# Summing the softmax denominators of the last attention unit: GpSimd adds replaced by accumulating DMAs

## The chip, the cores and the metric

The kernel is one program on one NeuronCore of a Trainium2 chip. Its time is the device time of one execution in microseconds (us). The kernel before takes 1054.57 us, the median of 3 runs (1052.63 to 1055.07). The engines are TensorE (PE in the profile, its weight loads PEld), VectorE (DVE), ScalarE (ACT), GpSimd (POOL) and SyncE (SP, which only issues DMAs here).

## The reference: what is computed

One transformer block in float32 on x of shape (2, 1024, 512): attention with 16 heads of 32 and low-rank additions to its four weight matrices, residual, layer norm, then a mixture-of-experts feed-forward layer (8 experts of 704 hidden units, 256 slots each, and a shared one), residual, layer norm. What matters here is the attention's core:

```
scores = jnp.einsum('bhqd,bhkd->bhqk', q, k) * SCALE
attn = jax.nn.softmax(scores, axis=-1)
out = jnp.einsum('bhqk,bhkd->bhqd', attn, v)
```

The softmax divides by the sum of the exponentials over all 1024 keys. The kernel applies this division after the product with v: it sums the exponentials beside it and scales the product.

## The kernel before

**Units and steps.** Attention's second pass is cut into 16 units (NU): a unit is 4 heads and 512 queries. A unit has 8 steps of 128 keys, so there are 128 steps; step t belongs to unit t // 8. In step t, st_step (L611) does for each of the 4 heads one matmul of scores (L620, 128 keys x 512 queries) and on ScalarE its exponential (L629). The exponentials of two heads, a pair, share one tile of 128 x 1024, pts[t, pair]. In the same step, av_step(t - 1) (L633) multiplies the exponentials of the step before with v (L639), adding up in one PSUM bank over the unit's eight steps. The tiles pts come from a pool of 14 buffers (PTB). The first pass (L189, L197), which finds row maxima, runs 12 steps ahead of the second and so is over by step 116.

**The denominators.** They need the sum of pts over the 8 steps and over the 128 partitions. Matmuls with a matrix of ones do the sum over partitions (finish, L666, matmuls at L672), and what of the eight tiles has been added together before saves such matmuls. The adds are spread by a table, ADDS (L62), by unit and step within the unit; adds(t) (L648) is called in step t + 1, right after av_step(t). A word of the table has two letters, for pair 0 and pair 1, and the number of a tile: b makes this tile the accumulator, v adds it to the accumulator on VectorE, p does that on GpSimd, and d starts a DMA that adds the tile into the next one:

```
accs[u, pr] = pts[i, pr]                                                    # b
pool.dma_start(out=pts[i + 1, pr], in_=pts[i, pr], accum_op=ALU.add)        # d, L656
eng.tensor_tensor(accs[u, pr], accs[u, pr], pts[i, pr], ALU.add)            # v, p: L659
```

Such an accumulating DMA is issued by GpSimd and moves 512 KB between tiles in SBUF. It may start when the value matmuls have read the tile that it adds into. Tile 7 of a unit is not added: finish sums it directly (DIRECT), in all units but unit 14 (NO_DIR).

In unit 15, the last, table row NU - 1 makes tile 0 the accumulator (step 121); pair 0 of tiles 1 to 5 is added by VectorE and pair 1 by GpSimd (steps 122 to 126); VectorE adds both pairs of tile 6 (step 127). In unit 14 tile 1 is the accumulator, tiles 0, 2 and 4 go into their neighbours by DMA, and VectorE adds tiles 3, 6, 7 and 5, the last three in step 120.

**What follows a sum.** For units 13 to 15 (RDIR) finish takes VectorE's reciprocal of the sums (L682, 128 x 512). normalize (L706) then has three parts: VectorE scales the product (L711), a copy is rounded for the projection (L714 on VectorE for units 13 and 14, L716 on ScalarE for unit 15), VectorE takes the rest (L718). FINE and NRME (L78) set the step within unit 15 at which unit 14's finish and normalize are queued: steps 123 and 125. In finish's step the sum comes on TensorE after av_step, and its reciprocal on VectorE after adds. In normalize's step the first part stands ahead of that step's adds and the other two behind them.

**The end of attention.** After step 127 come av_step(127), adds(127), finish(15), the first part of normalize(15), and then the output projection of rows 0 to 127 of the second batch element (op10, L744), which needs unit 14 but not unit 15. The list TAIL (L83) sets the order behind it: rows 128 to 511 (o1 to o3) also need only unit 14, rows 512 to 1023 (o4 to o7) unit 15 too. In between, ScalarE rounds and GpSimd splits the shared expert's weights (s0 to s5, L562 and L568), whose tiles two buffers feed (loads by SyncE, L554: a load waits for the split two before it), and GpSimd sets up the router (w0, L470). Behind that the feed-forward layer runs to the end.

**Order.** All engines' instructions stay in the order in which the program writes them (manual_schedule with MAN2), each engine with a queue of its own. An instruction that waits holds up all behind it on its engine.

Of the kernel before, what the change touches and what calls it, by code (L numbers as in the profile page):

```python
# [20 lines left out]
NU = 16  # L21
# [41 lines left out]
    None: {0: "bb0", 2: "dd1", 3: "pp3", 4: "pp4", 5: "pp2", 6: "pp5", 7: "pp6"},  # L63
    NU - 3: {0: "bb0", 2: "dd1", 3: "pp3", 4: "pp4", 5: "pp2", 7: "dd6 pp5"},
    NU - 2: {1: "bb1 dd0", 3: "dd2", 5: "dd4", 6: "vv3", 7: "vv6 vv7 vv5"},
    NU - 1: {0: "bb0", 1: "vp1", 2: "vp2", 3: "vp3", 4: "vp4", 5: "vp5", 6: "vv6"},
}
OPROJ_AT = (65, 67, 69, 71, 73, 75, 77, 79)
RES_AT = tuple(8 * i + (2 if i % 2 else 6) for i in range(8)) + (70, 74, 86, 90, 100, 102, 106, 110)
# [5 lines left out]
W2_AT = {2: (0, 1), 3: (2, 3), 4: (4,), 5: (5,)}  # L75
MPJ, MPP = 0, 2
RDIR = NU - 3
FINE, NRME = 3, {NU - 2: 6, NU - 1: 5}  # L78
OPROJ1 = 0
NRM_DVE = (NU - 3, NU - 2)  # L80
ROOT_LAG, NORM_LAG = 1, 4
# [1194 lines left out]
```

## Time and profile before

| what | value |
|---|---|
| median of 3 runs | 1054.57 us |
| the profiled execution | 1057.79 us |
| its span, first to last instruction | 1056.1 us |
| its granted TensorE clock, mean | 0.992 |
| PE, DVE, ACT, POOL busy | 1030.1, 696.0, 527.1, 585.9 us |
| second pass of attention, first to last score matmul | 155.6 to 601.5 us |
| VectorE adds L659 from unit 14's first (575.6) on | 15 |
| GpSimd adds L659 in unit 15, first start and last end | 585.14 and 600.8 us |
| accumulating DMAs L656 in the whole kernel | 36 (median 6.4 us from issue to landing) |

Lines of a timeline are start, duration, engine, line of the code, operation, output<-input, shapes and the number of instructions merged into the row; in brackets stands how long the engine had been idle and who ended that. Tiles are named without numbers: pt is any pts, sm a sum, av a product with v, rc a reciprocal, op a projection. A score or value matmul of float32 shows as one or two passes (x). In the table of stretches each engine has its busy time with the number of instructions, and PEclk is the granted share of TensorE's full clock.

### The profile page before, as it was taken

What the parts mean: (1) busy time and instruction counts of PE and PEld (TensorE: products, weight loads), DVE (VectorE), ACT (ScalarE), POOL (GpSimd) and SP (SyncE); (2) the same over time, 40 slices, a digit from 0 to 9 for tenths busy, and PEclk for the clock granted to TensorE, in tenths of its full rate; (3) what the DMA queues carried; (4) which work ended last, traced back from release to release, by engine and by line L of the source; (5) the groups of instructions that cost most, each with busy time, mean ns of one, the idle gap of its engine ahead of it and who ended that gap; (6) DMA issues with size and microseconds to landing.
All of it is one profiled execution on the core that took longest, in us unless ns stands there. A gap on an engine that the chain in (4) does not pass through costs nothing. (4 is left out here: it accounts for less than half of the span.)

```text
span 1056.1 us, 16556 instructions
## 1 busy us (share of the span) xinstructions
PE 1030.1 (98%) x5994; PEld 742.5 (70%) x5994; DVE 696.0 (66%) x1191; ACT 527.1 (50%) x1023; POOL 585.9 (55%) x407
## 2 busy tenths in 40 slices
PE   8999999999999999999999889999999999999995
PEld 6888774444444456544444359899999999999994
DVE  7732788778888877778887974233522557777752
ACT  5422216666666655566666716222222447555552
POOL 4000006999999986979995655000050046766674
PEclk9999999999999999999999989999999999999998
DMA  9866863454646553535648123000073456777721
GB/s 294 278 225 212 253 194 91 91 135 104 137 93 148 119 127 81 126 85 123 146 115 184 21 60 111 21 21 20 21 244 107 130 175 232 254 249 245 259 84 60
DMA packets 85449, 149.83 MB, mean 142 GB/s; under 512 B 15428, under 2 KB 24132, under 8 KB 85368
## 3 DMA queue, kind: packets, MB, share of 16 engines
q1 hardware_dynamic: 76344, 117.31, 37.5%
q0 software_dynamic: 9024, 31.48, 12.4%
q8 instruction: 47, 0.77, 0.3%
q14 instruction: 34, 0.28, 0.1%
HBM read 95.83 MB, written 33.78 MB: 123 GB/s over the span
## 5 line engine op out<-in xcount | busy, mean ns | idle before, releaser
L197 DVE TENSOR_REDUCE mt<-s 128x1 f32<-128x512 f32 x512 | 323.9, 681 | 79.7 <-PE s L189 79.3
L659 POOL TENSOR_TENSOR pt<-pt,pt 128x1024 f32<-128x1024 f32 x143 | 350.7, 2918 | 6.7 <-ACT pt L629 6.4
L629 ACT ACTIVATE pt<-st 128x512 f32<-128x512 f32 x512 | 269.1, 602 | 130.4 <-PE st L620 117.0
L620 PE MATMUL st<-qs,ks 98*128 98x512 f32 x512 | 213.2, 427 | 1.7 <-ACT pt L629 1.0
L189 PE MATMUL s<-ks,qs 96*128 96x512 f32 x512 | 200.3, 398 | 1.0 <-DVE mt L197 1.0
L620 PEld LDWEIGHTS st<-qs,ks 98*128 98x128 f32 x512 | 95.6, 189 | 133.5 <-issue 93.1
L656 POOL DMA_DIRECT2D pt<-pt x36 | 33.3, 1113 | 174.4 <-PE st L620 165.0
L890 PE MATMUL h<-xthe,w13s 128*128 128x256 f32 x704 | 130.0, 284 | 0.0
L878 POOL TENSOR_TENSOR w2s<-w2r,w2s 128x512 fp32r<-128x512 f32 x42 | 65.9, 1590 | 93.9 <-ACT w2s L877 93.6
L189 PEld LDWEIGHTS s<-ks,qs 96*128 96x128 f32 x512 | 97.1, 190 | 20.3 <-DVE mt L197 5.6
L890 PEld LDWEIGHTS h<-xthe,w13s 128*128 128x128 f32 x704 | 110.7, 191 | 0.3
L890 PE MATMUL h<-xtle,w13s 128*128 128x256 f32 x352 | 100.3, 285 | 0.0
L639 PE MATMUL av<-pt,vt 128*32 128x512 f32 x512 | 75.3, 605 | 0.0
L1038 POOL DMA_INDIRECT xd_d<-x1a,slot_i x8 | 7.9, 984 | 110.4 <-DVE slot_i L1035 108.3
L639 PE MATMUL av<-pt,x1b 128*32 128x512 f32 x512 | 68.2, 605 | 0.0
L890 PEld LDWEIGHTS h<-xtle,w13s 128*128 128x128 f32 x352 | 67.4, 191 | 0.7
L934 PE MATMUL y<-w2s,hs 128*128 128x512 f32 x260 | 60.9, 390 | 0.1
L934 PEld LDWEIGHTS y<-w2s,hs 128*128 128x128 f32 x260 | 48.2, 188 | 10.2 <-DVE hs L916 0.5
L331 ACT ACTIVATE oh<-o,bqk_sb 128x512 fp32r<-128x512 f32 x32 | 22.0, 690 | 57.8 <-PE o L316 53.0
L316 PE MATMUL o<-xh,wh 128*128 128x512 f32 x116 | 45.5, 392 | 0.3 <-DVE ol L332 0.3
L901 ACT ACTIVATE sl<-h 128x256 f32<-128x256 f32 x40 | 15.4, 385 | 60.5 <-PE h L890 59.2
L316 PE MATMUL o<-xh,wl 128*128 128x512 f32 x116 | 45.4, 391 | 0.0
(830 smaller groups left out, 1846.8 us busy)
## 6 DMA issues: line engine op xcount, KB each, us to landing
pt<-pt POOLq DMA_DIRECT2D x36, 512.0 KB, 6.4
x1a<-in_w_dram SPq DMA_DIRECT2D x24, 512.0 KB, 5.1
w2r<-in_w_dram SPq DMA_DIRECT2D x42, 256.0 KB, 3.4
qkd<-oh SPq DMA_DIRECT2D x32, 256.0 KB, 2.4
qkd<-ol SPq DMA_DIRECT2D x32, 256.0 KB, 2.4
x1b<-in_w_dram SPq DMA_DIRECT2D x16, 512.0 KB, 5.6
qs<-qkd SPq DMA_DIRECT2D x30, 256.0 KB, 4.5
ks<-qkd SPq DMA_DIRECT2D x18, 256.0 KB, 4.5
```

Of the source, the lines that this page charges most:

```text
L189: pe.matmul(s1, Qs[u % 3][0:96, h, qt * P : qt * P + P], Ks[g % 2][0:96, h, kh * 512 : kh * 512 + 512], start=True, stop=True,)
L197: dve.tensor_reduce(mts[u][:, c, kh : kh + 1], s1, AX.X, ALU.max)
L316: pe.matmul(o, lhs, rhs, start=k + i == 0, stop=k + i == KC + 1)
L331: act.activation(oh, o, AF.Identity, bias=bias)
L620: pe.matmul(sb, Ks[g % 2][:, h, kc * P : kc * P + P], Qs[u % 3][:, h, :], start=True, stop=True,)
L629: act.activation(pts[t, h // 2][:, h % 2, :], sb, AF.Exp, scale=SCALE)
L639: pe.matmul(avs[u][32 * h : 32 * h + 32, :], vts[g][:, kc, 32 * h : 32 * h + 32], pts[t, h // 2][:, h % 2, :], start=kc == 0, stop=kc == 7 ...
L656: pool.dma_start(out=pts[i + 1, pr], in_=pts[i, pr], accum_op=ALU.add)
L659: eng.tensor_tensor(accs[u, pr], accs[u, pr], pts[i, pr], ALU.add)
L878: pool.tensor_tensor(hl[:, 1, :], raw, f(hl[:, 0, :]), ALU.subtract)
L890: pe.matmul(hp[:, j * 256 : j * 256 + 256], lhs, rhs[:, k, :], start=n == 0, stop=n == 11,)
L934: pe.matmul(o, lhs, rhs, start=n == 0, stop=n == 16)
```

## The change

Row NU - 1 of the table of adds is written anew, and two constants become one step smaller.

```
-    NU - 1: {0: "bb0", 1: "vp1", 2: "vp2", 3: "vp3", 4: "vp4", 5: "vp5", 6: "vv6"},
+    NU - 1: {1: "bb1 dd0", 3: "dd2", 4: "vv4", 5: "vv5", 6: "vv3 vv6"},
...
-FINE, NRME = 3, {NU - 2: 6, NU - 1: 5}
+FINE, NRME = 2, {NU - 2: 6, NU - 1: 4}
```

In unit 15 tile 1 is now the accumulator. In step 122 GpSimd issues two DMAs that add tile 0 into tile 1 (one per pair), in step 124 two that add tile 2 into tile 3. VectorE adds both pairs of tile 4 (step 125), of tile 5 (step 126), and of tiles 3 and 6 (step 127). GpSimd adds nothing in this unit. Unit 14's finish is queued in step 122, its normalize in step 124. Everything else stays.

## The prediction

> **What bounds the kernel now.** I read the page first (TensorE busy 98% of the span), then the stretches around the end of attention:
>
> ```profile
> core 0: us, PE busy (x) PEld busy (x) DVE busy (x) ACT busy (x) POOL busy (x), PEclk, DMA share, GB/s
> 588.00:605.00 17.00, 16.35 (x79) 5.37 (x72) 16.86 (x10) 12.29 (x23) 11.99 (x5) 1.00 0.00 1
> 605.00:618.00 13.00, 6.72 (x19) 3.12 (x20) 10.87 (x5) 1.17 (x2) 9.24 (x28) 0.74 0.28 82
> 618.00:640.00 22.00, 22.00 (x108) 17.98 (x107) 15.71 (x37) 8.31 (x14) 10.21 (x11) 1.00 0.27 84
> ```
>
> Before and after the middle stretch TensorE is full at clock 1.00; in it TensorE works 6.72 of 13 us at clock 0.74, and VectorE is the busy engine. TensorE's waits from 575 to 640 name one cause:
>
> ```profile
> PE sm L672 <- DVE pt L659: 6.9, 3, 4.7
> ```
>
> Those are the denominators' sums (L672) waiting for the adds (L659). TensorE's timeline shows where, and what the idling does to the matmuls behind it:
>
> ```profile
> 589.51 1.05 PE L672 MATMUL sm<-pt,ones 128*32 128x512 f32 x4 [0.38 <-DVE pt L659]
> 590.50 0.73 PE L620 MATMUL st<-qs,ks 98*128 98x512 f32 x2
> ...
> 603.29 1.44 PE L672 MATMUL sm<-pt,ones 128*32 128x512 f32 x5
> 609.40 1.40 PE L672 MATMUL sm<-pt,ones 128*32 128x512 f32 x4 [4.67 <-DVE pt L659]
> 612.68 1.92 PE L672 MATMUL sm<-pt,ones 128*32 128x512 f32 x4 [1.88 <-DVE pt L659]
> 614.54 0.80 PE L744 MATMUL op<-wo_h,at_h 128*128 128x512 f32 x1
> ```
>
> TensorE is through with scores, values and the direct part of unit 15's sum at 604.73 (603.29 + 1.44); then it stands for the accumulator's two halves. The output projection (L744) starts at 614.54. From there to the end TensorE waits 0.3 us in all, so what this place loses or gains goes to the end. VectorE in the same time, then GpSimd:
>
> ```profile
> 575.64 1.22 DVE L659 TENSOR_TENSOR pt<-pt,pt 128x1024 f32<-128x1024 f32 x1
> 579.23 16.86 DVE L659 TENSOR_TENSOR pt<-pt,pt 128x1024 f32<-128x1024 f32 x9 [2.37 <-DMA pt<-pt]
> 596.02 3.34 DVE L682 RECIPROCAL rc<-sm 128x512 f32<-128x512 f32 x1
> 599.29 2.58 DVE L659 TENSOR_TENSOR pt<-pt,pt 128x1024 f32<-128x1024 f32 x1
> ...
> 604.85 7.78 DVE L659 TENSOR_TENSOR pt<-pt,pt 128x1024 f32<-128x1024 f32 x3
> ```
> ```profile
> 575.20 1.75 POOL L656 DMA_DIRECT2D pt<-pt  x2 [4.57 <-PE av L639]
> ...
> 585.14 6.55 POOL L659 TENSOR_TENSOR pt<-pt,pt 128x1024 f32<-128x1024 f32 x2 [5.84 <-ACT pt L629]
> 592.26 8.53 POOL L659 TENSOR_TENSOR pt<-pt,pt 128x1024 f32<-128x1024 f32 x3 [0.56 <-ACT pt L629]
> ```
>
> VectorE has no gap from 579.23 to 612.6. The same add takes very different times; the first row groups the 15 adds (minimum/median/maximum ns), the second the three that began between 586.0 and 593:
>
> ```profile
> L659 DVE TENSOR_TENSOR pt<-pt,pt x15: 1207/1224/3408, 575.6 to 609.3; 128x1024 f32<-128x1024 f32 x15
> ...
> L659 DVE TENSOR_TENSOR pt<-pt,pt 128x1024 f32<-128x1024 f32 x3 | 9.9, 3340 | 0.1
> ```
>
> It is 1.22 us alone and 3.3 us while GpSimd adds too (from 585.14 without much of a pause to 600.8), and again beside GpSimd's weight splits (L568, from 605.30). Until 585.14 GpSimd is quiet, and six VectorE adds in a row take 1.22 each.
>
> **The change, part by part.** Unit 15's five GpSimd adds go. VectorE's adds go from 7 to 8. Four accumulating transfers come in: pts[120] into pts[121] (step 122) and pts[122] into pts[123] (step 124), one per pair of heads. Unit 14's sum moves from step 123 to 122, its normalisation from 125 to 124. I follow VectorE and TensorE through the new order on the clock of the profiled execution.
>
> *Unit 14's accumulator.* Its eight adds and their transfers stay. Pair 0 is complete at 586.13 as now; pair 1's last add starts at 586.05 and now meets no GpSimd add, so 587.27 in place of 589.46.
>
> *Sum 14, a step sooner.* In step 122 it follows the value matmuls, which end at 586.1. Pair 0 runs at once; pair 1 waits until 587.3 and takes 0.99 (589.51 to 590.50), to 588.3. Step 122's next scores start at 588.3 instead of 586.10, 2.2 later. In exchange step 123 loses its sum: there it stretched the step from 2.7 (583.39 to 586.10) to 4.40, by 1.7. Net **+0.5 us** on TensorE. Behind the waiting sum in TensorE's queue are the scores of step 122, and behind those ScalarE's exponentials: all 0.5 later. The last exponential then ends at 603.3 (602.8 now).
>
> *VectorE.* Reciprocal 588.4 to 591.7 (3.34); normalisation of 14, three instructions of 0.69 (its high-part copy is VectorE's for this unit), to 593.9. Then unit 15: pts[124] by 596.5 (pair 1's exponentials end at 595.3), pts[125] by 599.1 (exponentials until 597.9), then pts[123] and pts[126], four adds of 1.15 to 1.22, if the second transfer has landed.
>
> *The transfers.* No exponential should wait for a buffer that they hold: in step 127 the live tiles are those of pts[121], [123], [126] and [127], eight of 14. On GpSimd each issue takes 0.86 to 1.2 us; nothing of weight is queued behind them (the next GpSimd work is the weight split after ScalarE's last exponential, 605.8 then). Like the present pairs they start only when the value matmuls have read the destination: 586.2, and 593.9 (value matmuls of step 123 at 592.1 plus 1.65). Landing, min/median/max, for the pair at 555 and for that at 575, which queued behind a late one:
>
> ```profile
> DMA to landing us min/median/max: 4.5/5.4/6.4
> ...
> DMA to landing us min/median/max: 6.5/7.4/8.4
> ```
>
> The new pairs have empty queues (the DMA share from 588 to 605 is 0.00), so I take 4.5 and 6.4 from each one's own issue: first pair landed by 593.4, before its reader at 593.9; second pair at 598.4 and 600.8. The upper bound is the largest of all 36, 9.7. So pts[123] pair 0 is added at 599.1 to 600.3, pair 1 at 600.8 to 602.0, pts[126] to 603.2 and **604.3**. This lies 1 us ahead of TensorE, whose direct part ends at 604.73 + 0.5 = 605.2.
>
> One rule of the Trainium skill speaks against this: SBUF — State Buffer, "SBUF: two separate sides", says that a transfer issued from GpSimd can be starved of descriptors while VectorE holds the shared port. By it the pair at 593.9 could write none before VectorE's run of adds pauses at 599.1; landing 603.6 and 605.5, adds ready at 607.9 and 609.0, 3.9 us lost. The row says otherwise: the pair issued at 575.20 lay on a VectorE add of the same form (575.64, 1.22 us, not slowed) and its two issues took 0.86 and 1.19, against 0.87 and 1.20 at 555.8, beside reductions that read PSUM. I take the row; the rule's price is kept for the range.
>
> *Sum 15 and behind it.* Its accumulator part starts at 605.2 without a wait and takes about 0.92 (eight passes; 16 take 1.90 at 568.17 in unit 13): projection at 606.1 in place of 614.54. That is 6.55 of waits (4.67 + 1.88) and 2.34 of slow passes (604.73 to 614.54 is 9.81, less 6.55, less 0.92), less the 0.5. Also the first six projection matmuls take 2.52 (614.54 to 617.06) where six at the later pace of 0.235 take 1.41: 1.1 more. TensorE: Matmul & The Clock Gate (Part 1) says that an idle window of about 3.4 us halves the clock until a busy one has passed; with no wait the clock stays up, and waits of 1 to 3 us (the rivals) would cost no slow matmuls, where this trace, with one of 4.67, can't tell.
>
> Sum: 6.55 + 2.34 + 1.1 - 0.5 = **9.5 us**.
>
> *Does the tail follow?* TensorE then has 48 projection matmuls that need unit 14 only (done 593.9), until 617.4. Unit 15's reciprocal (606.1 to 609.5), scaling, ScalarE's copy and VectorE's rest after the first row's statistics end at about 612.7: 4.7 us to spare (6.6 now). GpSimd's splits start 0.5 later but take 2.4 instead of 2.96 and 3.32, so SyncE's next weight loads (L554), which wait for them, come at 608.2 and 610.6 instead of 608.3 and 611.6; the router weights behind them at 611, and ScalarE waits for those about 2 us in front of nothing urgent (its next transposes come at 617). I cost all this at nothing; if it were in the open, 2 us.
>
> The execution with the profile took 1057.79 (span 1056.1), 3.2 above the median of 1054.57. 1057.79 - 9.5 = 1048.3; from the median, **1045.1 us**.
>
> **The rivals.**
> - *The second transfer is late* and its add becomes the wait in place of GpSimd's. With 9.7 us landing is at 604.1, the adds end at 606.5 and 607.6, projection at 608.6: gain 7.0, 1047.6. With starvation, 5.6: 1049.0. For it: only 1 us of slack. Against it: empty queues. 0.15.
> - *The tail gives part back*: some wait that 8 us of idle TensorE hid (weights, router set-up, banks), 2 to 5 us: about 1049. Against it: the slacks above. 0.08.
> - *It does nothing measurable*: VectorE's adds stay slow because something besides GpSimd slows them. Then eight adds of 3.3 end no sooner than 612. The 1.22 rows from 579 to 585, with scores, values and exponentials running, speak against it. 1054. 0.03.
> - *Slower*: the accumulating transfers of step 124 hold the end. Place: the add of pts[123] pair 1. Its landing L plus three adds (3.5) plus the last passes (1.4) is when projection starts; it loses from L = 609.6 on, and shows as slower from 611.7, i.e. when a transfer issued at 594.4 takes over 17 us, or when exponentials stall for buffers that transfers hold. At L = 612.5 it is 1057.4. The largest landing is 9.7, so 0.04.
> - *Forecast as summed*: 0.70.
>
> **How the numbers follow.** About 0.2% (2 us) is what can be told from no change. Faster by more than that: 0.70 + 0.15 + 0.08 = 0.93; same 0.03; slower 0.04. The range: below, 1045.1 less the spread of the runs shown (2 us down) is 1043; above, the late-transfer and give-back cases to 1049.5.
>
> **What would show it.** In the changed profile: VectorE's adds all near 1.22 us; no GpSimd add from 580 to 605; TensorE's waits for the sums under 2 us in all, most of it in step 122; projection about 9 us sooner; clock 1.00 across. I am wrong if the adds stay above 2 us, if a wait on an accumulating transfer stands before VectorE's last four adds, or if TensorE gets new waits after the projection.

## The result and the profile after

The changed kernel takes **1049.72 us** (median of 6 runs, 1048.84 to 1051.0); beside it the kernel before takes 1054.18 us (6 runs, 1051.86 to 1058.11). The ratio is 0.9957 [0.9936, 0.9977]: 4.5 us faster, where 9.5 were forecast. The profiled executions differ by nearly twice as much: 1057.79 before, 1048.99 after (span 1047.3, mean clock 0.996).

The table of stretches (busy us of PE, PEld, DVE, ACT, POOL, then PEclk, DMA share, GB/s) and TensorE's waits for the sums, after:

```profile
588.00:605.00 17.00, 17.00 (x86) 6.28 (x85) 14.79 (x12) 12.76 (x24) 1.75 (x2) 1.00 0.54 105
605.00:618.00 13.00, 13.00 (x62) 9.60 (x55) 9.13 (x16) 3.90 (x7) 9.68 (x31) 1.00 0.29 82
```
```profile
PE sm L672 <- DVE pt L659: 1.1, 1, 1.1
```

TensorE is full at clock 1.00 where it worked 6.72 of 13 us before, and of 6.9 us of waits 1.1 is left, at unit 14's sum. Its timeline, after:

```profile
586.49 2.19 PE L672 MATMUL sm<-pt,ones 128*32 128x512 f32 x8 [1.09 <-DVE pt L659]
588.61 1.20 PE L620 MATMUL st<-qs,ks 98*128 98x512 f32 x4
...
604.13 2.30 PE L672 MATMUL sm<-pt,ones 128*32 128x512 f32 x13
606.37 0.50 PE L744 MATMUL op<-wo_h,at_h 128*128 128x512 f32 x1
...
607.87 0.39 PE L744 MATMUL op<-wo_h,at_h 128*128 128x512 f32 x1
```

The projection starts at 606.37 and its seventh matmul at 607.87 instead of 617.06. VectorE and then GpSimd, after:

```profile
576.03 11.54 DVE L659 TENSOR_TENSOR pt<-pt,pt 128x1024 f32<-128x1024 f32 x8 [1.11 <-DMA pt<-pt]
588.72 3.36 DVE L682 RECIPROCAL rc<-sm 128x512 f32<-128x512 f32 x1 [1.16 <-PE sm L672]
...
594.18 1.22 DVE L659 TENSOR_TENSOR pt<-pt,pt 128x1024 f32<-128x1024 f32 x1
595.66 2.36 DVE L659 TENSOR_TENSOR pt<-pt,pt 128x1024 f32<-128x1024 f32 x2 [0.26 <-issue]
598.31 2.36 DVE L659 TENSOR_TENSOR pt<-pt,pt 128x1024 f32<-128x1024 f32 x2 [0.29 <-ACT pt L629]
600.84 3.50 DVE L659 TENSOR_TENSOR pt<-pt,pt 128x1024 f32<-128x1024 f32 x3 [0.17 <-DMA pt<-pt]
```
```profile
575.56 2.97 POOL L727 TENSOR_TENSOR x1b<-x1b,bo_bc 128x512 f32<-128x512 f32 x2
585.14 1.77 POOL L656 DMA_DIRECT2D pt<-pt  x2 [6.61 <-PE av L639]
593.82 1.75 POOL L656 DMA_DIRECT2D pt<-pt  x2 [6.91 <-PE av L639]
```

Unit 15's adds end at 604.34, each about 1.2 us. Only the first add of unit 14 is long (3.59): GpSimd's two residual adds (L727) began 0.47 us ahead of it. This row turned out to matter. VectorE also stood 0.17 us for the second transfer before its last three adds, a wait of the kind that I had named as a sign of being wrong; TensorE's last sum still had none.

For the comparison of executions I use the *stretch* from the issue of step 118's transfer (575.20 before, 574.44 after) to the projection's seventh matmul: **41.86 us before, 33.43 after**. (The two traces differ by 0.76 us at its start, so I compare the forecast's times by their distance from it.) What lies behind it is 439.0 us before and 439.4 after (1056.1 - 617.06, 1047.3 - 607.87), so the tail followed.

### The profile page after: what moved, and what is told of

Same layout as the page of the kernel before. It is cut to its first block, busy times and chain, and to the rows that moved or that the text cites. A ratio compares the mean times of both kernels' runs of the same rounds, so it can differ in the third digit from the quotient of the medians.

```text
span 1047.3 us, 16557 instructions
## 1 busy us (share of the span) xinstructions
PE 1026.7 (98%) x5994; PEld 741.5 (71%) x5994; DVE 687.7 (66%) x1192; ACT 527.2 (50%) x1023; POOL 573.2 (55%) x406
## 5 line engine op out<-in xcount | busy, mean ns | idle before, releaser
L659 POOL TENSOR_TENSOR pt<-pt,pt 128x1024 f32<-128x1024 f32 x138 | 336.0, 2917 | 0.1
L656 POOL DMA_DIRECT2D pt<-pt x40 | 36.9, 1101 | 187.2 <-PE st L620 164.2
L934 PEld LDWEIGHTS y<-w2s,hs 128*128 128x128 f32 x260 | 48.2, 188 | 10.2 <-DVE hs L916 0.5
L316 PE MATMUL o<-xl,wh 128*128 128x512 f32 x116 | 45.3, 390 | 0.1
```

The costliest lines, as they stand in the source:

```text
L316: pe.matmul(o, lhs, rhs, start=k + i == 0, stop=k + i == KC + 1)
L934: pe.matmul(o, lhs, rhs, start=n == 0, stop=n == 16)
```

## The experiments

My theory by now: the forecast's mechanism is right, but the stretch of the one traced execution is not that of every execution of the kernel before. Rivals: the gain is lost again elsewhere, or one of the two edits costs what the other brings. The first four kernels ran on one chip, on which the kernel before takes 1067.31 us (37 runs, 1063.11 to 1072.59).

**e1: the kernel before once more.** No edit.

> The kernel before once more, unchanged: how much of its profiled time is typical? The traces of before and after differ by 9.2 us where I forecast it (from step 118's accumulating DMA to the projection's seventh matmul: 41.9 us before, 33.4 after), the medians by only 4.5. Theory 1, the stretch itself varies: in most executions of before it is 3 to 5 us shorter than in the one that was profiled (VectorE and GpSimd block each other by chance of issue order, and whether TensorE falls to half clock depends on it); then a new trace has it at 36 to 39 us unless it happens to be a slow one, the time of the runs goes with their granted clock (about 0.996 in the fast ones, 0.992 in the slow), and their spread stays 5 us or more. Theory 2, the stretch is always near 42 and the profiled execution of before was slow elsewhere: a new trace has 41 to 43 there, and the difference to the median sits before 575 us or after 617.

Measured: 1.0002 [0.9982, 1.0022]; 14 runs from 1063.2 to 1073.66. The traced execution (1064.08) has a stretch of 36.45, not 41.86, and another course. TensorE in e1:

```profile
588.91 1.05 PE L672 MATMUL sm<-pt,ones 128*32 128x512 f32 x4 [0.72 <-DVE pt L659]
592.20 1.66 PE L672 MATMUL sm<-pt,ones 128*32 128x512 f32 x4 [2.23 <-DVE pt L659]
593.79 2.08 PE L620 MATMUL st<-qs,ks 98*128 98x512 f32 x4
...
606.98 2.55 PE L672 MATMUL sm<-pt,ones 128*32 128x512 f32 x13
609.46 0.50 PE L744 MATMUL op<-wo_h,at_h 128*128 128x512 f32 x1
```

The waits lie at unit 14's sum (3.0 us and slow passes behind them), and the last sum waits for nothing. Why, VectorE and GpSimd of e1 show:

```profile
575.95 18.65 DVE L659 TENSOR_TENSOR pt<-pt,pt 128x1024 f32<-128x1024 f32 x10 [0.96 <-DMA pt<-pt]
594.52 3.35 DVE L682 RECIPROCAL rc<-sm 128x512 f32<-128x512 f32 x1
```
```profile
575.64 2.98 POOL L727 TENSOR_TENSOR x1b<-x1b,bo_bc 128x512 f32<-128x512 f32 x2
584.47 6.60 POOL L659 TENSOR_TENSOR pt<-pt,pt 128x1024 f32<-128x1024 f32 x2 [5.85 <-ACT pt L629]
```

Unit 14's first add needs an accumulating transfer that was issued earlier. In the first trace it began at 575.64, 0.44 us after step 118's issue and 0.68 ahead of GpSimd's residual adds (576.32), and took 1.22. In e1 it waited for the transfer, began at 575.95, 1.43 us after the issue and behind the residual adds (575.64), and took 3.76. I call an add that is held up in this way *blocked*, the other one *free*. So VectorE's seventh add comes at 585.45, *behind* GpSimd's first add (584.47), and with the eighth takes 3.4 each; in the first trace it came at 584.92, 0.22 us *ahead* of GpSimd (585.14), and only the eighth was slow. Unit 14's sum then waits; meanwhile scores and exponentials stand still, GpSimd has nothing to add from 591.1 to 595.85, VectorE catches up, and the last sum finds its adds done. I call the first trace's way course one, this one course two.

**e2: the new row of adds alone.**

```
-    NU - 1: {0: "bb0", 1: "vp1", 2: "vp2", 3: "vp3", 4: "vp4", 5: "vp5", 6: "vv6"},
+    NU - 1: {1: "bb1 dd0", 3: "dd2", 4: "vv4", 5: "vv5", 6: "vv3 vv6"},
```

> The new row of adds alone; unit 14's sum and normalisation stay in steps 123 and 125. If the gain is GpSimd's adds no longer slowing VectorE's: at least the whole gain, ratio to before 0.994 to 0.9965, and 0.5 to 1 us under the whole change, since the sum of unit 14 then finds its adds done (they ended at 587.6 in the trace of the change, and step 123's sum comes at 588) and TensorE's wait of 1.1 us in step 122 is gone. If the earlier sum and reciprocal carry the gain: ratio near 1.000, with VectorE's reciprocal late and a wait of several us at the last sum.

Measured: 0.993 [0.9909, 0.9952], 1061.01 us; TensorE waits for neither sum; stretch 31.58. This came about although unit 14's first add was blocked (4.16 us): its sum stands a step later than in the whole change, and the adds are done in time.

**e3: the earlier steps alone**, with the old row.

```
-FINE, NRME = 3, {NU - 2: 6, NU - 1: 5}
+FINE, NRME = 2, {NU - 2: 6, NU - 1: 4}
```

> The earlier sum and normalisation of unit 14 alone, with the old row of adds (five GpSimd adds in unit 15). If GpSimd's adds are the cause of the loss: no gain, ratio 0.999 to 1.002, VectorE's adds still 2 to 3.4 us beside GpSimd's, TensorE's wait for the sums 6 to 9 us in all, with 2 to 3 us of it moved to step 122. If the earlier reciprocal carries the gain: ratio 0.995 to 0.998.

Measured: 0.9978 [0.9964, 0.9992], a small gain where I expected none. TensorE in e3:

```profile
588.59 1.05 PE L672 MATMUL sm<-pt,ones 128*32 128x512 f32 x4 [2.23 <-DVE pt L659]
589.57 1.20 PE L620 MATMUL st<-qs,ks 98*128 98x512 f32 x4
...
605.05 3.34 PE L672 MATMUL sm<-pt,ones 128*32 128x512 f32 x13
```

One wait of 2.23 at unit 14's sum, no slow passes behind it, none at the last: stretch 35.50. Waits of 6 to 9 us were expected: a miss. The first add was free here (1.23), as in the first trace, whose stretch was 41.86, but as in course two the wait came at unit 14's sum, GpSimd then had nothing to add for a while (587.45 to 591.38), and the last sum found its adds done.

**e4: the whole change once more.**

> The change once more, to have a second trace and more times beside the others. Both theories: 1049 to 1050 us, ratio 0.994 to 0.998, a narrow spread (about 2 us); the stretch from step 118's DMA to the projection's seventh matmul 33 to 34 us. Theory 2 would be helped by a trace in which the rest of the change's run is 3 to 5 us longer than the rest of a typical run of before.

Measured: 0.9946 [0.9927, 0.9964], 1062.56 us; a wait of 1.57 at unit 14's sum; stretch 33.89, as expected. The runs were not (1060.44 to 1065.01, where 1049 to 1050 was expected): on this chip every kernel takes longer. The row alone has the lower median, but the runs of the two overlap.

The next four ran on a second chip (kernel before 1067.42 us, 35 runs, 1063.56 to 1072.17) and were to force the courses.

**e5: course two forced**, by eight small memsets on VectorE ahead of unit 14's third add.

```
+            if t == 119:
+                for _ in range(8):
+                    dve.memset(pad, 0.0)
```

> The kernel before with eight tiny memsets (128 x 16) on VectorE between the second and third add of unit 14, about 0.5 us of delay. The two traces of before differ by where TensorE waits: in one VectorE's last add but one of unit 14 began 0.2 us before GpSimd's first add of unit 15, and the wait (6.6 us, then half clock) stood at the last sum; in the other it began 1 us after it, two adds were slowed, and the wait (3.0 us) stood at unit 14's sum, with none at the last one. Theory 1 (before has two courses, chosen by this race): the delay puts all executions on the second course: wait of 2 to 5 us at unit 14's sum, under 1 us at the last sum, ratio to before 0.996 to 0.9995 although work was added, spread of the runs smaller than before's 9 us. Theory 2 (the differences between executions of before lie elsewhere): ratio 1.000 to 1.001 and the same spread.

Measured: 1.0001 [0.9983, 1.0019]; the 14 runs lie within 3.4 us (1066.41 to 1069.77), where the 35 of the kernel before lie within 8.6. TensorE in e5 (lines shifted by 4):

```profile
592.97 3.06 PE L676 MATMUL sm<-pt,ones 128*32 128x512 f32 x8 [3.73 <-DVE pt L663]
```

The course and the narrow spread came as expected, with a stretch of 37.56; the lower time did not. In this trace the first add had been blocked by the residual adds as well (4.45 us), so the course would probably have been two without the memsets.

**e6: course one forced by leaving an add out.** Pair 1 of unit 14's last tile isn't added, so that unit 14's sum lacks it.

```
-    NU - 2: {1: "bb1 dd0", 3: "dd2", 5: "dd4", 6: "vv3", 7: "vv6 vv7 vv5"},
+    NU - 2: {1: "bb1 dd0", 3: "dd2", 5: "dd4", 6: "vv3", 7: "vv6 v-7 vv5"},
```

> The kernel before without VectorE's add of pair 1 of unit 14's last tile (two heads' denominators lack 128 of 1024 keys, so this leaves work out); VectorE is 1.1 us sooner from there. Theory 1: all adds of unit 14 but at most one are over when GpSimd starts, so executions take the first course: no wait at unit 14's sum, 5 to 9 us at the last sum, ratio to before 1.000 to 1.005 although an add is gone. Theory 2: 0.998 to 1.000.

Measured: 1.0002 [0.9978, 1.0026], 1062.45 to 1074.74, so not narrowed. A miss: the traced execution took course two in spite of the missing add. The first add was blocked here too (2.90), and VectorE's second add, which waits for another transfer, began only at 581.25 (579.23 in the first trace). TensorE in e6 (lines shifted by 2), with the same single wait as e3, but slow passes behind it:

```profile
589.25 1.05 PE L674 MATMUL sm<-pt,ones 128*32 128x512 f32 x4
592.54 1.92 PE L674 MATMUL sm<-pt,ones 128*32 128x512 f32 x4 [2.23 <-DVE pt L661]
594.39 1.90 PE L620 MATMUL st<-qs,ks 98*128 98x512 f32 x4
```

**e7: all of unit 15's adds on VectorE, no accumulating transfers.**

```
-    NU - 1: {0: "bb0", 1: "vp1", 2: "vp2", 3: "vp3", 4: "vp4", 5: "vp5", 6: "vv6"},
+    NU - 1: {0: "bb0", 1: "vv1", 2: "vv2", 3: "vv3", 4: "vv4", 5: "vv5", 6: "vv6"},
```

> All of unit 15's adds on VectorE (14 in all, without GpSimd and without accumulating DMAs; unit 14's sum stays in step 123). If what matters is that GpSimd adds nothing beside VectorE: adds of 1.22 us throughout, last one at about 607, TensorE's wait at the last sum 1 to 2 us, most of the gain: ratio 0.995 to 0.9975, 1 to 2 us above the new row alone. If the accumulating DMAs carry the gain: ratio near 1.000.

Measured: 1.0013 [0.9994, 1.0032], no gain, where most of the gain was expected: a miss. (Unit 15 has 12 adds on VectorE here, not the 14 that I wrote; with unit 14's 8 the trace shows 20.) The rows of VectorE and GpSimd, then TensorE, in e7:

```profile
603.19 6.78 DVE L659 TENSOR_TENSOR pt<-pt,pt 128x1024 f32<-128x1024 f32 x4
606.27 2.61 POOL L568 TENSOR_TENSOR w13s-1_0_6235<-w13r,w13s-1_0_6235 128x1024 fp32r<-128x1024 f32 x1 [25.11 <-ACT w13s-1_0_6235 L562]
```
```profile
606.73 1.05 PE L672 MATMUL sm<-pt,ones 128*32 128x512 f32 x4 [1.03 <-DVE pt L659]
610.02 1.05 PE L672 MATMUL sm<-pt,ones 128*32 128x512 f32 x4 [2.24 <-DVE pt L659]
611.00 0.79 PE L744 MATMUL op<-wo_h,at_h 128*128 128x512 f32 x1
```

Unit 15's adds are 1.2 us but for the last, which takes 3.37 beside GpSimd's first weight split. The four transfers relieve VectorE of four adds and let it end before the splits begin.

**e8: a third trace of the kernel before.** No edit, one execution.

> A third trace of the kernel before, with the time of that execution. Theory 1: one of the two courses: either a wait of 5 to 7 us at the last sum and a time in the upper half of the runs of before, or 2 to 4 us at unit 14's sum, about none at the last, and a time in the lower half. Theory 2: the waits don't go with the time.

Measured: 1066.29 us, course two again: the first add began 1.36 us after the issue and took 3.82, waits of 0.57 and 2.23 at unit 14's sum, none at the last; stretch 36.56.

The last four ran on a third chip (kernel before 1064.81 us, 53 runs, 1061.08 to 1070.19).

**e9: course one forced**, by holding up GpSimd's first add of unit 15 for about 3.6 us.

```
+            if t == 121:
+                pool.tensor_copy(pad, pts[t, 1][:, 1, 0:16])
+                for _ in range(15):
+                    pool.memset(pad, 0.0)
```

> The kernel before with a tiny copy and fifteen tiny memsets on GpSimd ahead of its first add of unit 15, so that this add starts 2 to 3 us later, after VectorE's last add of unit 14. Theory 1 (the race between these two decides the course): every execution takes the course of the first trace: no wait or under 0.5 us at unit 14's sum, 4 to 8 us of wait at the last sum, and times in the upper group of the runs of before (which fall into two groups with a gap of 1.5 us between them), ratio 1.001 to 1.005, spread under 6 us. Theory 2: ratio 0.999 to 1.001 and the two groups as before.

Measured: 1.0023 [1.0008, 1.0037], 1068.36 us; a stretch of 38.26. The narrow spread didn't come (1064.43 to 1072.77). TensorE in e9:

```profile
606.50 1.05 PE L677 MATMUL sm<-pt,ones 128*32 128x512 f32 x4 [1.76 <-DVE pt L664]
609.78 1.92 PE L677 MATMUL sm<-pt,ones 128*32 128x512 f32 x4 [2.23 <-DVE pt L664]
611.63 0.80 PE L749 MATMUL op<-wo_h,at_h 128*128 128x512 f32 x1
```

All eight adds of unit 14 take 1.22, its sum waits for nothing, and the loss is at the last sum: 4.0 us of waits, with slow passes and a slow projection. So the waits went where course one has them. What course one costs by itself this doesn't show, since the hold-up also delays GpSimd's adds: the last one ends 29.3 us after step 118's issue (605.36 - 576.10) instead of 25.6 (600.79 - 575.20). Nor is it shown that the runs of the kernel before fall into two groups, as the expectation says: the gap of 1.5 us is in the 37 runs of the chip of e1 to e4 (1067.82 to 1069.36), three of e1's own runs lie in it (1068.9 to 1069.25), and the samples of the other two chips have none over 0.8.

**e10: e7 with GpSimd's first splits behind ScalarE's copy of unit 15.**

```
-    "l0 l1 t0 s0 s1 n1 n2 w0 ...
+    "l0 l1 t0 n1 s0 s1 n2 w0 ...
```

> Unit 15's adds all on VectorE, as in the kernel with VectorE alone, but ScalarE's rounding of the projection input of unit 15 is queued ahead of the first two weight splits, so that GpSimd splits nothing until the last sum is done. There the last add of 3.37 us lay on GpSimd's split of 606.27 to 608.88. If that collision ate the gain: all adds 1.2 us, wait at the last sum 1 to 2 us in all, projection 2 us sooner, ratio to before 0.996 to 0.9985. If VectorE's fourteen adds are too many by themselves: ratio 0.999 or more.

Measured: 0.9998 [0.9979, 1.0017]. TensorE's waits in e10:

```profile
PE op L744 <- DVE x1b L749: 3.2, 1, 3.2
PE sm L672 <- DVE pt L659: 2.2, 1, 2.2
```

The slow add is gone and the stretch 2.2 shorter than in e7 (34.43 against 36.67), but it is given back: the router weights' load is issued behind the late splits, ScalarE waits 7.7 us for it, VectorE 8.2 for ScalarE, and TensorE 3.2 for VectorE.

**e11 and e12: the row alone and the whole change once more**, as e2 and e4, to be compared with e9.

> The new row of adds with unit 14's sum and normalisation left in steps 123 and 125, once more beside the whole change, since their intervals overlapped. Expected: ratio 0.992 to 0.995, and 1 to 2 us under the whole change; no wait of TensorE at either sum.

> The whole change beside it: ratio 0.994 to 0.997; one wait of 1 to 2 us at unit 14's sum in step 122.

Measured: e11 0.9933 [0.9908, 0.9958], 1057.88 us; e12 0.9965 [0.9953, 0.9977], 1061.36 us. Stretches 31.57 and 32.48. In e12 unit 14's first add is free (577.23, before the residual adds at 577.72; 1.23 us), where in the first trace of the change (3.59) and in e4 (2.77) it was blocked. In e11 it is blocked (3.59), and TensorE still waits for neither sum. Unit 14's adds and sum and the end of attention in e11:

```profile
576.08 11.54 DVE L659 TENSOR_TENSOR pt<-pt,pt 128x1024 f32<-128x1024 f32 x8 [1.12 <-DMA pt<-pt]
587.67 1.32 PE L672 MATMUL sm<-pt,ones 128*32 128x512 f32 x6
...
601.75 2.86 PE L672 MATMUL sm<-pt,ones 128*32 128x512 f32 x13
604.54 0.50 PE L744 MATMUL op<-wo_h,at_h 128*128 128x512 f32 x1
```

On both chips on which it was tried the row alone is ahead of the whole change, by 1.6 us (1062.56 - 1061.01) and 3.5 us (1061.36 - 1057.88); the first is within the spread of the runs. The stretches differ by 2.3 (33.89 - 31.58) and 0.9 (32.48 - 31.57). It is the best version of this study.

## Why the prediction went wrong, point by point

**Right: what slows the adds.** Without GpSimd's adds, unit 15's are 1.2 us, and e7 shows the other side: one GpSimd operation of the same size on the last of them, and that one takes 3.37.

**Right: the transfers, the last sum, the tail.** The new transfers were issued in 0.86 and 1.21 us and landed 4.5 and 6.4 us later, the values taken, at 598.29 and 600.75. The second pair lay on VectorE's adds from 594.18 on, and the starvation that I had weighed did not show. (The Trainium skill, SBUF — State Buffer, "SBUF: two separate sides", says it of VectorE's operations in a 2-port mode, such as a copy; I had applied it to adds.) Sum 15 had no wait, the tail followed, and ScalarE's wait for the router weights (3.6 us) cost nothing.

**Right for one course only: unit 14's accumulator and sum.** Forecast was the end of that sum 13.1 us after step 118's issue (588.3 - 575.20). In e12 it is 13.2 (589.80 - 576.61), in the first trace of the change 14.2 (588.61 - 574.44): there the blocked first add pushes the accumulator back by 1 us, and the sum has the wait of 1.09. I had taken the first add's 1.22 from the first trace, where it won its race by 0.68 us, and had not asked what it costs when it loses. The sum of 9.5 holds for the free case: 41.86 - 9.5 = 32.36, measured 32.48 in e12. Its three large terms are also borne out by the row alone, without the early sum: 41.86 - 6.55 - 2.34 - 1.1 = 31.87, measured 31.57 and 31.58; the rest, 0.3, is about the wait of 0.38 that I left aside.

**Wrong: "from the median, 1045.1".** This step carries 3.2 us of the miss of 4.6 (1049.72 - 1045.1); the blocked first add carries about 1 (33.43 instead of 32.36). I saw that the profiled execution stood 3.2 us above the median, and above the highest of three runs, and subtracted its loss from the median all the same. That assumes that the median execution loses as much in this stretch. Two of the three traces of the untouched kernel do not: their stretch is 36.5. Like with like, the stretch gains 41.86 - 32.48 = 9.4 us with a free first add and 36.5 - 33.43 = 3.1 (36.5 - 33.89 = 2.6 in e4) with a blocked one. The measured 4.5 lies between, as do 3.45 and 4.75 on the other chips (1064.81 - 1061.36, 1067.31 - 1062.56). The wait and the slow matmuls of course two were in the kernel before all along, but at another sum, 3 us of them instead of 6.9. Set against one execution, the forecast fared better: 1057.79 - 9.5 = 1048.3, and the profiled execution after took 1048.99. Part of that is luck: the stretch was 1.1 us longer than forecast, but the time ahead of it happened to be 0.8 shorter.

Shown is that the kernel before has both courses, which wait each one takes, and in its three traces that the one with a free first add took course one and the two with a blocked one course two; e5 and e6, both blocked, took course two as well. A free first add doesn't settle the course by itself: e3, with the earlier sum, had one and took the other way.

How often the race goes which way can be counted, since none of the edits changes an instruction ahead of unit 14's first add. In the fourteen traces it was free in five (the first one, e3, e7, e9, e12) and blocked in nine, and on each of the four sets of runs, the first one included, both came about; so a chip doesn't settle the outcome. An estimate from these counts and the two gains, (5 x 9.4 + 9 x 3.1) / 14, is 5.3 us, somewhat above the 3.5 to 4.8 measured.

Not shown is the course of a run without a trace, and the two traces of course two are from other chips than the result; that the median of the result's own runs lost less is inferred. Forcing gave only part of it: e9 was slower than the kernel before, but the hold-up itself may be the reason, and e5 was not faster, though its stretch is 4 us shorter than the first trace's. The time outside the stretch varies too: behind the projection's seventh matmul it is 439 us in the two traces of the result and 450 to 456.5 in the other twelve. Those twelve have, in the experts' matmuls, waits of TensorE of 5 to 9 us that the profile puts down to nothing it shows, and from about 770 us on a granted clock of 0.50 for 10.2 us (e1) to 13.7 us (e12); the first two have neither. Why is open. The two courses thus explain the sign and the rough size of the miss, not its last microsecond.

**Wrong, and free this time: what waits cost.** From the idle window of about 3.4 us that the Trainium skill gives (TensorE: Matmul & The Clock Gate, Part 1) I took waits of 1 to 3 us to cost no slow matmuls. In e1 0.72 and 2.23 us with four matmuls between them did: the next four scores took 2.08 instead of 1.20. A single 2.23 did so in e6 and not in e3, behind the same sum and beside the same matmuls. The granted clock shows the difference. In each trace the phases of half clock start whole multiples of 3.413 us apart (in e6 at 159.06, 592.55 and 773.46 us: 127 and 53 times), so a trace can be cut into slices of 3.41 us that begin with such a phase. Those around the wait, in e6 and then in e3, as rows of the table of stretches:

```profile
589.13:592.54 3.41, 1.18 (x5) 0.14 (x5) 3.41 (x3) 0.01 (x1) 2.27 (x1) 1.00 0.00 0
592.55:595.96 3.41, 3.41 (x8) 1.34 (x8) 3.31 (x3) 0.73 (x2) 0.00 (x0) 0.50 0.00 0
```
```profile
583.90:587.31 3.41, 2.43 (x12) 0.28 (x6) 3.41 (x3) 1.26 (x3) 3.05 (x1) 1.00 0.00 0
587.31:590.72 3.41, 2.13 (x10) 0.84 (x10) 3.39 (x3) 0.56 (x2) 0.14 (x1) 1.00 0.00 0
```

In e6 the wait lies within one slice, in which TensorE worked 1.18 us, and the next one has PEclk 0.50. In e3 it is cut in two at 587.31 (54 slices ahead of the half clock at 771.63), and PEclk stays 1.00. Between 560 and 630 us all traces agree: after a full-clock slice with 0.20 (e5) to 1.43 us of work (e10) comes half clock, after one with 1.59 (before) or more it doesn't. Elsewhere it came after 2.35 us too (e6, ahead of 159.06), so the limit isn't shown. What is shown is that a wait well below 3.4 us can cost slow matmuls, and that it is a matter of luck how it falls on the slices.

**The rivals.** None came about. The second transfer held VectorE for 0.17 us but TensorE not at all; behind the stretch the change took 0.4 us longer; "nothing measurable" and "slower" did not arise. A rival that was missing: that the loss in the trace is only one of two ways in which the kernel runs.

## What to carry to other kernels

Set a profiled execution's time beside the spread of the runs before subtracting what it shows: if it stands at the edge, the loss in it may not be every execution's, and a second trace of the same kernel is the cheapest experiment. Look in the trace for starts that lie a few tenths of a microsecond from a competitor's (here 0.68 us for one add and, as a consequence, 0.22 us for a later one), gated by a DMA: such a race can send later work down another course. And try the parts of a change alone: here the half that was to help along cost 3.5 us on one chip, and on another 1.6, within the spread.

## What the hardware showed unexpectedly

- When VectorE's and GpSimd's 128 x 1024 adds meet, both lose: VectorE's go from 1.22 to 3.4 us, GpSimd's from 2.38 (alone, in e1 at 595.85) to 3.2.
- A blocked add gets almost nothing done meanwhile: in all nine traces it ended 1.09 us after GpSimd's second residual add, whenever it had begun. One that starts just ahead of them can be caught as well: 0.49 us ahead it took 1.23 (e12), 0.38 us ahead 4.45 (e5). Against GpSimd's 128 x 1024 adds 0.22 us ahead was enough (first trace, 1.22).
- VectorE's reciprocal, which reads PSUM, keeps its 3.34 to 3.36 us beside GpSimd's adds; issuing transfers on GpSimd doesn't slow VectorE's adds.
- Slow matmuls followed waits of 2.8 us in all (e8), 3.0 (e1), 3.3 (e7), 3.7 (e5) and 4.0 (e9); after 2.2 in one piece they came once (e6) and twice not (e3, and e10, where the wait from 605.10 to 607.30 is cut at 606.71, 5 slices ahead of the half clock at 623.78).
